# Gathering a layer's first six pairs before its last block of nodes is stored, in a three-layer graph network

## The chip, the cores and the metric

The kernel runs on one core of a Trainium2 chip. The metric is the device time of one execution in microseconds (us); the time before is the median of three runs. The engines of the core are named PE (matrix products), DVE (vector engine), ACT (scalar engine), POOL (GpSimd) and SP (which only issues transfers). A transfer is issued from the queue of SP, ACT or GpSimd.

## The reference

There are 6,250 nodes with 256 features and 100,000 edges. Each edge has a source `src`, a destination `dst`, 32 attributes and one of three types. The edges come sorted by destination. Three layers run one after the other, and after them a layer norm of the input plus the result:

```python
ew = edge_attr @ edge_w + edge_b
for l in range(3):
    msg = relu(x[src] * ew)
    out = 0
    for i in range(3):
        h = segment_sum(msg * mask[i], dst) / max(count[i], 1)
        out = out + h @ weights[l, i]
    x = x + relu(out + x @ roots[l] + biases[l])
```

All data are fp32. The destinations crowd at low node numbers, so the first blocks of nodes receive the most edges. The sources are spread over all nodes: every layer's gather may need any row of `x`.

## The kernel before

**Tiling.** 128 edges are a tile, two tiles a pair (391 pairs), two pairs with one buffer `xs` a quad. Nodes are worked in 49 blocks of 128. The order of the pairs is written out by `schedule`: first pairs 64 to 390, then 63 down to 0. So the last pairs of a layer belong to blocks 1 and 0, and block 0 is the last block to be finished in a layer. Positions in this order are called p below.

**One pair.** `gather_pair` (L893) issues two indirect transfers from GpSimd, each of 128 rows of 1 KB of `x`: in layer 0 from the input, in layers 1 and 2 from `x_mid[l-1]` in device memory, which the layer before has stored. PE makes the edge weights `ew_p` (`make_ew`, L610). DVE multiplies them into the rows in place (`weigh`, L618; it reads `ew_p` from PSUM), ACT applies the relu (`bound`, L622). DVE makes one-hot matrices of 3 x 40 places from a row of counters (`one_hot`, L628). PE multiplies rows and one-hots (`reduce`, L638), which sums the messages by destination and type in a window of 40 nodes. DVE adds the window to a ring of sums `acc` (`add`, L656).

**One block.** `node_mul` (L684) multiplies the sums with the layer's weights into `o_p` or `r_p`; `node_end` (L715, L718) scales, adds the root part, the relu and the old `x`, and stores the block in `x_mid[l]` from SP (L720). The root part `x @ roots` is made earlier, in four steps (`root_turn`, `root_turned`, `root_mul`, `root_keep`; L661 to L672), and is kept in `x_root`, which has `ROOTS` = 28 places; `root_at` says at which step each block's root part is made, and a place is used again only when its block has been finished.

**Order.** Nothing is scheduled by a planner: the loop over `it` (L757) writes every engine's instructions out in order. At step `it` it issues the gather for position it + 9, the edge weights for it + 4, the weighing for it + 3, the one-hots for it + 2, the reduction for it, the addition for it - 1 (layer 0) or it - 2. Each engine works its own list in that order, and waits on semaphores where it needs another. GpSimd's list holds little but gathers, and it runs ahead of the others as far as the `xs` buffers allow (`ROWS` = 8). The first `FIRST` = 6 pairs of layer 0 are gathered earlier still (L983), while the kernel checks that the edges are sorted.

**A layer's end.** Block 0 is finished at the last steps: `node_mul` at step 391 (layer 0) or 392, `node_end` three steps later. Since a gather may read any row of `x_mid`, the next layer's first gather waits for the store of block 0.

Of the kernel before, what the change touches and what calls it, by code (L numbers as in the profile page):

```python
# [8 lines left out]
F32 = mybir.dt.float32  # L9
BF = mybir.dt.bfloat16  # L10
I32 = mybir.dt.int32
AF = mybir.ActivationFunctionType
ALU = mybir.AluOpType
# [426 lines left out]


@with_exitstack
def ordered_path(ctx, tc, x, edge_attr, weights, roots, biases, edge_w, edge_b, out, src_i, seg, place_i, consts, rows,
                 first_rows):

# [2 lines left out]
    nc = tc.nc  # L450
    P = 128
    N, D = x.shape
    E, A = edge_attr.shape
    L, R = weights.shape[:2]
    NT = (N + P - 1) // P
    T = (E + P - 1) // P
    T -= T % -2
    U = T // 2
# [4 lines left out]
    AHEAD = 9  # L463
    order, _, moved, least, most = schedule(N, E, 1)
# [8 lines left out]
    ident, ones, iota_w = consts  # L473
# [4 lines left out]
    x_mid = [dram.tile([N, D], F32, name=f"x_mid{l}") for l in range(L - 1)]  # L478

    big = ctx.enter_context(tc.tile_pool(name="big", bufs=1))  # L480
# [5 lines left out]
    x_all = big.tile([P, NT, D], F32, name="x_all")  # L486
# [20 lines left out]
                                 zero.to_broadcast([P, R * (ASIDE + 2 * P + WIN)]), AF.Copy)  # L507
    nc.vector.memset(x_all[:, NT - 1, :], 0.0)

    edge = ctx.enter_context(tc.tile_pool(name="edge", bufs=2))  # L510
    wpool = ctx.enter_context(tc.tile_pool(name="wpool", bufs=1))
    o_pool = ctx.enter_context(tc.tile_pool(name="o_p", bufs=1, space=PSUM))
# [5 lines left out]
    def first_of(p, n):  # L518
        return p == 0 or order[p - 1] // n != order[p] // n
# [24 lines left out]
    def load_root(l):  # L544
        r_sb = wpool.tile([P, DC, D], F32, name="r_sb")
        nc.sync.dma_start(r_sb, roots[l].rearrange("(c p) e -> p c e", p=P))
        b_sb = wpool.tile([P, D], F32, name="b_sb")
        nc.sync.dma_start(b_sb, biases[l:l + 1, :].to_broadcast([P, D]))
        return r_sb, b_sb
# [7 lines left out]
            nc.sync.dma_start(at[:, :pairs_in(g)].rearrange("p k e -> p (k e)"), at_all[g, :, :pairs_in(g) * P])  # L557
        return at

    def layer(l, r_sb, b_sb, ats, pools):  # L560
        h_pool = pools.enter_context(tc.tile_pool(name="h_p", bufs=2 if l == 0 else 3, space=PSUM))
        ew_pool = pools.enter_context(tc.tile_pool(name="ew_p", bufs=3, space=PSUM))
        if l == 0:
# [7 lines left out]
        CH = DC + 1 if l == 0 else DC  # L571
        xs, ew_ps, ohs, h_ps, turns, o_ps, rs = {}, {}, {}, {}, {}, {}, {}
        x0s, mvs, oh_bs, t_ss, places = {}, {}, {}, {}, []
        r_next, ats_next = (None, None), {}

        def gather(u):
            p = order.index(u)
            if l == 0 and p < FIRST:
                xs[u // 2] = first_rows[u // 2]
            else:  # L580
                if first_of(p, 2):
                    xs[u // 2] = room(rows, D)
                gather_pair(nc, xs[u // 2], x_rows, src_i, u)
# [20 lines left out]
        def make_ew(q):  # L604


            ew_ps[q] = {i: ew_pool.tile([P, 2, D], F32, name="ew_p") for i in (1, 0)}
            for k in pairs_of(q):
                for i in range(2):
                    nc.tensor.matmul(ew_ps[q][i][:, k, :],  # L610
                                     ats[2 * q // GROUP][i * UP:i * UP + A1, (2 * q + k) % GROUP, :],
                                     ew_sb[i * UP:i * UP + A1, :], start=True, stop=True)

        def weigh(q):
            n = len(pairs_of(q))
            for i in (1, 0):
                there = xs[q][:, :n, i, :]
                nc.vector.tensor_mul(there, ew_ps[q][i][:, :n, :], there)  # L618
# [138 lines left out]
        for it in range(-11, max(starts) + 7):  # L757
            def pair(k):
                return order[it + k] if 0 <= it + k < U else None
            if pair(AHEAD) is not None:  # L760
                gather(pair(AHEAD))
            if l == 0 and pair(11) is not None and first_of(it + 11, 4):
                load_attrs(pair(11) // 4)
            if l > 0 and pair(AHEAD) is not None and pair(AHEAD) // GROUP not in ats:
                ats[pair(AHEAD) // GROUP] = load_at(l, pair(AHEAD) // GROUP)
            if l == 0 and it >= -4 and (it + 4) % 20 == 0 and (it + 4) // 20 * 6 < NT - 1:
                load_x((it + 4) // 20 * 6)
            if it == 10:
                nc.sync.dma_start(w_sb, weights[l].rearrange("r (c p) e -> p (r c) e", p=P))
            if l == L - 1 and it + 2 in root_at:  # L770
                load_x0(root_at[it + 2])
            if l < L - 1 and it == U - 10:
                r_next = load_root(l + 1)
            if l < L - 1 and U <= it < U + 2:
                ats_next[at_groups[it - U]] = load_at(l + 1, at_groups[it - U])

            if pair(4) is not None and first_of(it + 4, 2):
                make_ew(pair(4) // 2)
            if pair(0) is not None:
                reduce(pair(0))  # L780
            if pair(-LAG) is not None:
                add(pair(-LAG))
            if pair(3) is not None and first_of(it + 3, 2):
                weigh(pair(3) // 2)
                bound(pair(3) // 2)
            if l == 0:

                for k, work in ((6, keep_attrs), (7, turn)):
                    if pair(k) is not None and first_of(it + k, 2):
                        work(pair(k) // 2)  # L790
                if pair(4) is not None and last_of(it + 4, GROUP):
                    store_at(pair(4) // GROUP)
            if it in root_at:
                root_turn(root_at[it])
            if it - 1 in root_at:
                root_turned(root_at[it - 1])
            if it - 2 in root_at:
                root_mul(root_at[it - 2])
            if it - 3 in root_at:
                root_keep(root_at[it - 3])  # L800
            if it == moved:
                move()
            if it - 2 == moved:
                clear(P)
            if it + 1 in node_at and slot_of(node_at[it + 1]) == 0:
                wrap()
            if it in node_at:
                node_mul(node_at[it], 0)
            if it - 1 in node_at:
                node_end(node_at[it - 1], 0)  # L810
            if it - 2 in node_at:
                node_mul(node_at[it - 2], 1)
            if it - 3 in node_at:
                node_end(node_at[it - 3], 1)
                clear(slot_of(node_at[it - 3]))
            if it - 4 in node_at and l == L - 1:
                deviate(node_at[it - 4])
            if it - 5 in node_at and l == L - 1:
                norm(node_at[it - 5])
            if pair(2) is not None and first_of(it + 2, 2):  # L820
                one_hot(pair(2) // 2)
        return (*r_next, ats_next)

    with tc.manual_schedule():
        state = (*load_root(0), {})
        for l in range(L):
            with ExitStack() as pools:
                state = layer(l, *state, pools)
# [5 lines left out]
WIN = 40  # L834
RING = 1024
ASIDE = RING + WIN
ROOTS = 28
GROUP = 8
ROWS = 8
FIRST = 6  # L840
# [47 lines left out]
def room(rows, D):  # L888

    return rows.tile([128, 2, 2, D], F32, name="xs", bufs=ROWS)  # L890


def gather_pair(nc, xs, x_rows, src_i, u):  # L893
    for i in range(2):
        nc.gpsimd.indirect_dma_start(  # L895
            out=xs[:, u % 2, i, :], out_offset=None, in_=x_rows[:, :],
            in_offset=bass.IndirectOffsetOnAxis(ap=src_i[:, 2 * u + i:2 * u + i + 1], axis=0))
# [3 lines left out]
def kernel(ctx, tc, x, src, dst, edge_attr, edge_type, weights, roots, biases, edge_w,  # L901
# [3 lines left out]
    nc = tc.nc  # L905
    P = 128
    N, D = x.shape
    E = src.shape[0]
    NT = (N + P - 1) // P
# [5 lines left out]
    U = T // 2  # L915
# [3 lines left out]
    keep = ctx.enter_context(tc.tile_pool(name="keep", bufs=1))  # L919
    ident = keep.tile([P, P], F32, name="ident_o")  # L920
    make_identity(nc, ident)
    ones = keep.tile([1, P], F32, name="ones_o")
    nc.vector.memset(ones, 1.0)
    iota_w = keep.tile([P, WK], F32, name="iota_w")
    nc.gpsimd.iota(iota_w, pattern=[[1, WK]], base=0, channel_multiplier=0,
                   allow_small_or_imprecise_dtypes=True)
    src_i = keep.tile([P, TC], I32, name="src_io")
    seg = keep.tile([P, TC], F32, name="seg_o")
    place_i = keep.tile([1, (U + 1) // 2], I32, name="place_i")
    flag = keep.tile([1, 1], I32, name="flag")  # L930
    rows = ctx.enter_context(tc.tile_pool(name="rows", bufs=ROWS))

    with tc.tile_pool(name="look", bufs=1) as look, tc.tile_pool(name="look_p", bufs=2, space=PSUM) as look_p, \
            tc.manual_schedule():
        full, rest = divmod(E, P * J)
# [46 lines left out]
        first_rows = {}  # L982
# [52 lines left out]

    unordered = nc.values_load(flag[0:1, 0:1], min_val=0, max_val=1)
    with tc.If(unordered == 0):
        ordered_path(tc, x, edge_attr, weights, roots, biases, edge_w, edge_b, out, src_i, seg, place_i,
                     (ident, ones, iota_w), rows, first_rows)
    with tc.If(unordered > 0):  # L1040
        general_path(tc, x, src, dst, edge_attr, edge_type, weights, roots, biases, edge_w, edge_b, out)

# [25 lines left out]
```

## Time and profile before

| | |
|---|---|
| median of three runs | 3025.5 us (3022.97 to 3029.19) |
| the profiled execution | 3023.81 us, its span 3021.9 us |
| granted PE clock over the span | 0.932 |
| PE, PE's weight loads | 2792.5 us (92%), 2263.6 us (75%) |
| GpSimd | 2235.7 us (74%), 2354 instructions, nearly all gathers |
| DVE | 2071.2 us (69%) |
| ACT | 987.0 us (33%) |
| gathers of layer 0, and of layers 1 and 2 | 782 and 1564, mean 952 ns each |
| PE clock from 1000 to 1050 us and from 2000 to 2050 us | 0.73 and 0.70 |

A line of the order of time gives start and duration in us, engine, line, operation, `out<-in`, and in brackets the idle time of the engine before it with what ended it; several equal instructions are merged, so the duration of "x8" is that of all eight together. A product of fp32 operands shows as two instructions. "issue" means that the engine waited for nothing that the profile shows. In a line of the costliest groups, the numbers after the bar are the busy time in us, the mean of one in ns, and the idle time in front of the group with its largest cause. Matmul ends are modelled, so a busy PE need not be at its peak. The layers' borders lie near 1016 and 2013 us.

### The profile page before, as it was taken

What the parts mean: (1) busy time and instruction counts of PE and PEld (TensorE: products, weight loads), DVE (VectorE), ACT (ScalarE), POOL (GpSimd) and SP (SyncE); (2) the same over time, 40 slices, a digit from 0 to 9 for tenths busy, and PEclk for the clock granted to TensorE, in tenths of its full rate; (3) what the DMA queues carried; (4) which work ended last, traced back from release to release, by engine and by line L of the source; (5) the groups of instructions that cost most, each with busy time, mean ns of one, the idle gap of its engine ahead of it and who ended that gap; (6) DMA issues with size and microseconds to landing.
All of it is one profiled execution on the core that took longest, in us unless ns stands there. A gap on an engine that the chain in (4) does not pass through costs nothing. (4 is left out here: it accounts for less than half of the span.)

```text
span 3021.9 us, 55648 instructions
## 1 busy us (share of the span) xinstructions
PE 2792.5 (92%) x18066; PEld 2263.6 (75%) x18066; DVE 2071.2 (69%) x5841; ACT 987.0 (33%) x1354; POOL 2235.7 (74%) x2354
## 2 busy tenths in 40 slices
PE   6999999999999789999999999879899999999987
PEld 5787888888877567777777777767777777777776
DVE  6667777777776456666666667546667777778764
ACT  4444444445444222222222222212222222222221
POOL 6777777777777577777777777767777777777775
PEclk9999999999998889999999999768999999999997
DMA  5555555555555444444444445434444444444443
GB/s 150 169 167 162 163 163 153 153 151 159 160 151 153 128 126 137 138 131 141 134 141 144 143 137 151 150 105 149 150 149 145 151 148 137 148 141 145 139 139 95
DMA packets 274250, 437.82 MB, mean 145 GB/s; under 512 B 144956, under 2 KB 179728, under 8 KB 273952
## 3 DMA queue, kind: packets, MB, share of 16 engines
q0 software_dynamic: 112608, 307.65, 35.0%
q1 hardware_dynamic: 154720, 119.64, 12.8%
q10 hardware_dynamic: 6624, 6.87, 0.8%
q8 instruction: 149, 2.44, 0.3%
q14 instruction: 149, 1.22, 0.1%
HBM read 389.15 MB, written 44.82 MB: 144 GB/s over the span
## 5 line engine op out<-in xcount | busy, mean ns | idle before, releaser
L895 POOL DMA_INDIRECT xs<-x_mid,src_io x1564 | 1489.6, 952 | 509.6 <-issue 420.4
L638 PEld LDWEIGHTS h_p<-oh,xs 128*128 128x128 f32 x9384 | 1233.7, 207 | 235.8 <-issue 188.8
L638 PE MATMUL h_p<-oh,xs 128*128 128x120 f32 x9384 | 1366.7, 299 | 16.4 <-issue 8.1
L622 ACT ACTIVATE xs<-xs 128x1024 f32<-128x1024 f32 x588 | 620.3, 1055 | 1865.5 <-DVE xs L618 1779.8
L618 DVE TENSOR_TENSOR xs<-ew_p,xs 128x512 f32<-128x512 f32 x1176 | 753.7, 683 | 597.7 <-DMA xs<-x_mid,src_io 388.0
L610 PE MATMUL ew_p<-ew_sb,at 33*128 33x256 f32 x4692 | 859.0, 421 | 172.2 <-DVE xs L618 171.1
L895 POOL DMA_INDIRECT xs<-in_x_dram,src_io x782 | 744.4, 952 | 254.2 <-issue 203.8
L610 PEld LDWEIGHTS ew_p<-ew_sb,at 33*128 33x128 f32 x4692 | 503.0, 193 | 410.4 <-DVE xs L618 205.4
L656 DVE TENSOR_TENSOR acc<-h_p,acc 128x240 f32 (+1 forms) x1173 | 519.4, 443 | 211.7 <-PE h_p L638 117.6
L628 DVE TENSOR_SCALAR oh<-iota_w,seg_o 128x120 f32<-128x120 f32 x2346 | 517.2, 295 | 0.0
L684 PE MATMUL o_p<-w_sb,acc 128*128 128x256 f32 (+1 forms) x1716 | 441.2, 395 | 4.9 <-DVE acc L656 4.9
L684 PEld LDWEIGHTS o_p<-w_sb,acc 128*128 128x128 f32 (+1 forms) x1716 | 318.6, 198 | 41.7 <-DVE acc L656 6.3
L715 DVE SCALAR_TENSOR_TENSOR x_root<-o_p,inv,x_root 128x256 f32<-128x256 f32 (+1 forms) x429 | 206.1, 480 | 52.6 <-PE o_p L684 45.0
L669 PE MATMUL r_p<-r_sb,t_s 128*128 128x256 f32 x588 | 162.6, 402 | 0.0
L701 ACT ACTIVATE acc<-zero_o 128x768 f32<-128x768 f32 (+1 forms) x150 | 140.6, 937 | 38.4 <-PE r_p L684 20.2
L632 ACT ACTIVATE oh_b<-oh 128x480 bf16<-128x480 f32 x196 | 117.9, 602 | 92.7 <-DVE oh L628 91.6
L669 PEld LDWEIGHTS r_p<-r_sb,t_s 128*128 128x128 f32 x588 | 108.2, 205 | 9.2
L638 PE MATMUL h_p<-oh_b,full_ones 128*128 128x120 bf16 x782 | 108.0, 221 | 0.0
L594 PE MATMUL turn_p<-ident_o,an 128*128 128x128 f32 x391 | 79.9, 287 | 10.7 <-DMA an<-in_edge_attr_dram 6.0
L638 PEld LDWEIGHTS <-full_ones 128*128 128x128 bf16 x782 | 82.6, 106 | 2.9
L672 DVE TENSOR_TENSOR x_root<-r_p,b_sb 128x256 f32<-128x256 f32 x147 | 61.4, 418 | 32.7 <-PE r_p L669 31.4
L602 ACT ACTIVATE at<-turn_p 128x256 f32<-128x256 f32 x196 | 71.5, 365 | 1.5 <-PE turn_p L594 1.4
(88 smaller groups left out, 487.4 us busy)
## 6 DMA issues: line engine op xcount, KB each, us to landing
at<-at_all SPq DMA_DIRECT2D x96, 512.0 KB
xs<-x_mid,src_io POOLq DMA_INDIRECT x1564
at_all<-at SPq DMA_DIRECT2D x48, 512.0 KB
xs<-in_x_dram,src_io POOLq DMA_INDIRECT x782
an<-in_edge_attr_dram SPq DMA_DIRECT2D x97, 128.0 KB
x_mid<-x_all SPq DMA_DIRECT2D x96, 128.0 KB
x_all<-in_x_dram ACTq DMA_DIRECT2D x8, 768.0 KB
x<-in_x_dram SPq DMA_DIRECT2D x48, 128.0 KB
```

Of the source, the lines that this page charges most:

```text
L610: nc.tensor.matmul(ew_ps[q][i][:, k, :], ats[2 * q // GROUP][i * UP:i * UP + A1, (2 * q + k) % GROUP, :], ew_sb[i * UP:i * UP + A1, :], st ...
L618: nc.vector.tensor_mul(there, ew_ps[q][i][:, :n, :], there)
L622: nc.scalar.activation(there, there, AF.Relu)
L628: nc.vector.tensor_scalar(ohs[q][:, t, :], iota_w, seg[:, 4 * q + t:4 * q + t + 1], None, op0=ALU.is_equal)
L632: nc.scalar.activation(oh_bs[q][:, :n], ohs[q][:, :n], AF.Copy)
L638: nc.tensor.matmul(h_ps[u][:, d, :], xs[u // 2][:, u % 2, i, d * P:(d + 1) * P] if d < DC else full_ones, (ohs if d < DC else oh_bs)[u // ...
L656: nc.vector.tensor_tensor(there, h_ps[u][:, :CH].rearrange("p c (r w) -> p c r w", r=R), there, op=ALU.add)
L669: nc.tensor.matmul(rs[c][:, 1, :], t_ss[c][:, d, :], r_sb[:, d, :], start=(d == 0), stop=(d == DC - 1))
L684: nc.tensor.matmul(o_p[:n, j, :], acc[:, d, r, slot:slot + n], w_sb[:, r * DC + d, :], start=(d == 0), stop=(d == DC - 1))
L701: nc.scalar.activation(acc[:, :CH, :, slot:slot + P], zero[:, :, None, None].to_broadcast([P, CH, R, P]), AF.Copy)
L715: nc.vector.scalar_tensor_tensor(root, o_p[:n, j, :], inv[:n, c, r:r + 1], root, op0=ALU.mult, op1=ALU.add)
L895: nc.gpsimd.indirect_dma_start(out=xs[:, u % 2, i, :], out_offset=None, in_=x_rows[:, :], in_offset=bass.IndirectOffsetOnAxis(ap=src_i[:, ...
```

## The change

`x_mid` gets zeros in its first 128 rows at the start of the kernel, by two stores from ACT's queue. In layers 0 and 1 the loop issues the next layer's first six pairs of gathers (12 transfers) right behind the layer's own last ones, at steps U - 9 to U - 4, into `xs` buffers that are handed to the next layer. At that time all blocks but block 0 have been stored, so an edge whose source lies in block 0 receives zeros. The store of block 0 comes after these gathers.

In the next layer, `complete` adds what is missing, ahead of the weighing of each of the first three quads. For every tile, PE multiplies a 128 x 128 matrix `came` (1 where the edge's source is that node of block 0) with block 0's new rows, which stand in `x_all[:, 0, :]`; DVE adds the product to the gathered rows. The products take turns in the single buffer `o_p`, two tiles at a time.

`came` is made once, at step 20 of layer 0: a transfer on ACT's queue brings the 1,536 sources of these pairs to all 128 partitions, and DVE compares them with the partition's number, in 12 instructions. It takes 6 KB of each partition, and `ROOTS` goes from 28 to 24.

```diff
@@ ordered_path
+    for rows_of in x_mid:
+        nc.scalar.dma_start(rows_of[:P, :], x_all[:, NT - 1, :])
+    came = big.tile([P, 2 * FIRST, P], F32, name="came")
+    came_i = came.bitcast(I32)
...
+    def find_came():
+        e = 2 * P * order[0]
+        nc.scalar.dma_start(came_i.rearrange("p t e -> p (t e)"),
+                            src[e:e + 2 * FIRST * P][None, :].to_broadcast([P, 2 * FIRST * P]))
+        for t in range(2 * FIRST):
+            nc.vector.tensor_scalar(came[:, t, :], came_i[:, t, :], node_i[:, 0:1], None, op0=ALU.is_equal)
+
-    def layer(l, r_sb, b_sb, ats, pools):
+    def layer(l, r_sb, b_sb, ats, early, pools):
...
         def gather(u):
             p = order.index(u)
-            if l == 0 and p < FIRST:
-                xs[u // 2] = first_rows[u // 2]
+            if p < FIRST:
+                xs[u // 2] = early[u // 2]
...
+        def gather_early(p):
+            u = order[p]
+            if first_of(p, 2):
+                early_next[u // 2] = room(rows, D)
+            gather_pair(nc, early_next[u // 2], x_mid[l], src_i, u)
+
+        def complete(q):
+            for k in pairs_of(q):
+                rest = o_pool.tile([P, 2, D], F32, name="o_p")
+                for i in range(2):
+                    nc.tensor.matmul(rest[:, i, :], came[:, 4 * q + 2 * k + i - 2 * order[0], :], x_all[:, 0, :],
+                                     start=True, stop=True)
+                nc.vector.tensor_add(xs[q][:, k], rest, xs[q][:, k])
...
             if pair(AHEAD) is not None:
                 gather(pair(AHEAD))
+            if l < L - 1 and 0 <= it + AHEAD - U < FIRST:
+                gather_early(it + AHEAD - U)
+            if l == 0 and it == 20:
+                find_came()
...
             if pair(3) is not None and first_of(it + 3, 2):
+                if l > 0 and it + 3 < FIRST:
+                    complete(pair(3) // 2)
                 weigh(pair(3) // 2)
                 bound(pair(3) // 2)
...
-        return (*r_next, ats_next)
+        return (*r_next, ats_next, early_next)
...
-ROOTS = 28
+ROOTS = 24
@@ tile_gnn_resnorm_kernel
+    node_i = keep.tile([P, 1], F32, name="node_i")
+    nc.gpsimd.iota(node_i, pattern=[[0, 1]], base=0, channel_multiplier=1, allow_small_or_imprecise_dtypes=True)
```

## The prediction

> **What bounds the kernel now.** I read the costliest groups first, then the order of time at the two layer boundaries, then the start of layer 0, where the change also puts work.
>
> ```profile
> L895 POOL DMA_INDIRECT xs<-x_mid,src_io x1564 | 1489.6, 952 | 509.6 <-issue 420.4
> L638 PE MATMUL h_p<-oh,xs 128*128 128x120 f32 x9384 | 1366.7, 299 | 16.4 <-issue 8.1
> L618 DVE TENSOR_TENSOR xs<-ew_p,xs 128x512 f32<-128x512 f32 x1176 | 753.7, 683 | 597.7 <-DMA xs<-x_mid,src_io 388.0
> ```
>
> PE is busiest (92%), but DVE's weighing waited 388.0 us for gathers, and a gather is followed by 0.30 us of "issue" only. In the order of time the gathers start 1.25 us apart: 0.95 of work and 0.30 of issue. A layer has 782, so 978 us; layer 2's run from 2015.13 to 2999.11 (984). GpSimd's gathers set the pace, and the other engines follow with little lag. GpSimd stops for long only at the boundaries:
>
> ```profile
> 999.92 0.94 POOL L895 DMA_INDIRECT xs<-in_x_dram,src_io  x1 [0.30 <-issue]
> 1011.48 1.13 PE L684 MATMUL o_p<-w_sb,acc 128*128 128x256 f32 x4 [0.63 <-DVE acc L656]
> 1015.89 0.42 DVE L718 SCALAR_TENSOR_TENSOR x_all<-x_root,x_all 128x256 f32<-128x256 f32 x1
> 1016.34 0.32 SPq L720 DMA_DIRECT2D x_mid<-x_all  x1
> 1019.04 0.94 POOL L895 DMA_INDIRECT xs<-x_mid,src_io  x1 [18.17 <-issue]
> 1025.70 1.29 DVE L618 TENSOR_TENSOR xs<-ew_p,xs 128x512 f32<-128x512 f32 x2 [9.39 <-DMA xs<-x_mid,src_io]
> ...
> 2012.14 0.42 DVE L718 SCALAR_TENSOR_TENSOR x_all<-x_root,x_all 128x256 f32<-128x256 f32 x1
> 2015.13 0.94 POOL L895 DMA_INDIRECT xs<-x_mid,src_io  x1 [14.66 <-DMA x<-in_x_dram]
> 2021.69 1.29 DVE L618 TENSOR_TENSOR xs<-ew_p,xs 128x512 f32<-128x512 f32 x2 [9.12 <-DMA xs<-x_mid,src_io]
> 2029.55 3.77 PE L638 MATMUL h_p<-oh,xs 128*128 128x120 f32 x16
> ```
>
> Read it as: last gather of a layer; block 0 finished on DVE (T = 1016.31 and 2012.56); its store; first gather of the next layer 2.73 and 2.57 us after T, after 18.17 and 14.66 us of idling; first weighing 9.4 and 9.1 us after T. The 12 early gathers need 12 x 1.25 = 15.0 us, so they fit the hole.
>
> **How far gathers may run ahead** decides whether that gain is kept. Of eight row buffers three stay with the first rows; in the built program the gather of a quad waits until PE has reduced the fifth quad before it, before and after the change. The start of layer 0 shows it:
>
> ```profile
> 50.02 0.95 POOL L895 DMA_INDIRECT xs<-in_x_dram,src_io  x1 [0.31 <-issue]
> 55.80 1.11 PE L638 MATMUL h_p<-oh,xs 128*128 128x120 f32 x8
> 57.67 0.94 POOL L895 DMA_INDIRECT xs<-in_x_dram,src_io  x1 [6.70 <-issue]
> ```
>
> The 33rd gather (ninth quad) starts 0.76 us after the eighth pair's reduction, which ends the fourth quad (56.91).
>
> **Gathers and store at a boundary.** At the first, early gathers start at 1001.17, the twelfth at 1014.9; a gather's rows are used 2.92 us after its start (1022.78 to 1025.70), so it lands at 1017.85. The store of block 0 now also waits for all of them: issue 1.5 us late. Behind it on SP stand a load of at and w_sb, not due before about 1040. The next gather comes 2.70 us after the store, at 1020.6. At the second boundary: 2000.77, landed 2017.4, next gather about 2020.0. The first gather of pair 6 stood at 1034.0 and 2030.1, so GpSimd could gain 13.4 and 10.1.
>
> **Completion, on the way of the consumers.** Three quads each need, twice in turn (one o_p buffer): two products from 128x256 (four instructions: 1.13 in the row above, 1.93 at half clock, at 2053.13), then a DVE addition of 128x512 (0.68, from L618's 683 ns). Then comes the first weighing (0.65). The chain from T to the end of quad 1's reduction, which frees the buffer for quad 6:
> - full clock: completion and weighing 1.13+0.68+1.13+0.68+0.65+0.25 of hand-offs = 4.5, for three quads 13.5; ew remainders (six of eight instructions) 3 x 0.9; two quads' reductions of 2.04 each = 4.1. Together 20.3, so quad 6 is gathered at T + 21.0. From GpSimd's own pace it could start 15 us after the restart: T + 19.3 and T + 22.5. It started at T + 32.7 and 32.6 before. Gain 11.7 and 10.1.
> - half clock from the second quad on: 4.5 + 1.63 + 6.1 + 1.63 + 3.77 + 5.3 to 6.1 + 0.9 to 1.63 + 2.04 to 3.77 = 25.9 to 29.1; with 0.76, T + 26.7 to 29.9. Gain 2.7 to 6.0.
>
> Here the Trainium skill speaks ("TensorE: Matmul & The Clock Gate", Part 1): the clock halves after an idle window of about 3.4 us and returns after a busy one. No gap in the chain is over 1.5 us, so the rule would give the full clock and some 22 us in all. The trace is harsher: PE idled 1.27 us before 2048.00, and the next quad's reduction (16 instructions) took 3.77 us, as at 2029.55, instead of the 2.04 of 2039.93. PE's granted clock was 0.54 from 1016.3 to 1034 and 0.79 just before. The measurement decides: half clock for most of the chain, and its upper end, 5 us per boundary, since PE is nearly full from the second reduction on. Sum: -10. Afterwards consumers can do a quad in about 4.1 us (2038.55 to 2046.73 for two) against 5.0 of gathers, so the gain stays.
>
> **Finding the one-hots, in layer 0.** DVE comes to its 12 comparisons right after a weighing, with the 786 KB transfer only just issued behind ACT's bounding:
>
> ```profile
> 82.70 1.29 DVE L618 TENSOR_TENSOR xs<-ew_p,xs 128x512 f32<-128x512 f32 x2 [1.75 <-DMA xs<-in_x_dram,src_io]
> 84.02 1.06 ACT L622 ACTIVATE xs<-xs 128x1024 f32<-128x1024 f32 x1 [3.90 <-DVE xs L618]
> 84.34 0.85 DVE L628 TENSOR_SCALAR oh<-iota_w,seg_o 128x120 f32<-128x120 f32 x4
> 87.67 2.00 POOL L895 DMA_INDIRECT xs<-in_x_dram,src_io  x1 [0.30 <-issue]
> 93.74 0.95 POOL L895 DMA_INDIRECT xs<-in_x_dram,src_io  x1 [0.30 <-issue]
> ```
>
> The nearest transfer is x_all's, as large, issued at 74.05 on the same queue; its packets end at 79.73: D = 5.7 us. Comparisons: 12 x 0.21 (0.85/4) = 2.6. Queued behind them on DVE: an addition (0.53), which the reduction of pair 21 waits for (1.1), which the gather at 93.74 (quad 15) waits for (0.76). So that gather may start at 84.0 + D + 2.6 + 2.4 = 89.0 + D, a loss of D - 4.7: 1.0 us at D = 5.7, nothing under 4.7. PE then comes back at half clock while DVE pays its backlog: 2 us for the next buffer. I take 3; bounds 0 and 10, should 128 readings of the same 6 KB cost 12 us.
>
> The skill's page "SBUF — State Buffer" (Who interferes with whom) also speaks against the comparisons: such a DVE instruction in its two-port mode shuts GpSimd out, so 2.6 us more could be lost. The rows say less: the gather at 37.45, beside four L628, took 1.02 against 0.95; only the one beside a 1.35 us addition (87.51) took 2.00. I take 0.1.
>
> **The rest.** Two zero stores on ACT's queue wait for a memset of 30.11, under fills that last to 32.73: nothing, up to 0.7 without that cover. One more iota precedes an 8.74 us wait of GpSimd: nothing. 24 instead of 28 root buffers push root work from steps 131-163 to as late as 243 in each layer; four more blocks at 1.4 us of PE fall into layer 0's fullest part (PE 98 to 99%), where gathers lead by up to five quads: 1 us, bounds 0 and 3.
>
> **Sum**, on the profiled execution: 3023.81 - 10 + 3 + 1 = 3017.8. That execution lies 1.7 under the median of 3025.5, so the forecast there is 3019.
>
> **Rivals.**
> - PE keeps its clock: gains 11.7 and 10.1, cost 4: 3008. For it: PE is at full clock when block 0 ends (1.13 us row). Against: the 2048.00 row.
> - The completion takes the place of the wait: hand-offs and half clock leave 1 us or less per boundary, buffers let nothing through; with the 4 us, 3027. For it: six alternations of two engines, where before there was one wait. Against: even the half-clock sum ends before T + 32.
> - Slower: the broadcast transfer. Each us beyond D = 4.7 is lost, because layer 0's gathers have no slack to make it up. It decides from a loss of about 16 us (D near 20): 3035. For it: DVE stops outright. Against: 786 KB took 5.7.
> - The early gathers do not start in the hole (a buffer still held): the second early quad needs the third-last quad but one reduced, and PE is at the last three by 1001.6. Weak; 3029.
>
> **How the numbers follow.** Half-clock chain 0.5 (3019, own range 3012 to 3026), full clock 0.2, replaced wait or no early start 0.18, slow transfer 0.12. Under 0.2% (6 us) a measurement here hardly tells a difference. The bound for faster lies at 3019.4: half of the first case and all of the second, 0.45. Same: the rest of the first and the third, 0.41. Slower 0.14. Range 3004 to 3033: full clock at one end, most of the transfer case out.
>
> **What would show it.** Right: gathers at 1.25 us through 1001 to 1016; GpSimd idle then 4 to 5 us instead of 18.17 and 14.66; a second stop of GpSimd before the sixth or seventh quad; PE's granted clock near 0.6 after T; a gap of some us near 94 in layer 0. Wrong: a DVE stop near 84 of over 12 us; gathers of later quads stopped again through the layer; root work that holds PE between 455 and 625.

## The result, and the profile after

| | before | after |
|---|---|---|
| median time | 3025.5 us (3021.17 to 3030.12, 11 runs) | 3018.14 us (3011.54 to 3023.37, 11 runs) |
| ratio | | 0.9977 (95% interval 0.9970 to 0.9985) |
| span of the profiled execution | 3021.9 us | 3016.4 us |
| T: block 0 finished, boundary 1 and 2 | 1016.31, 2012.56 | 1020.67, 2009.61 |
| quad 12 gathered, after T | 62.8, 62.9 us | 55.5, 61.8 us |

The change is a gain of 0.23%, some 7 us. The last row measures a boundary: by quad 12 all stops of GpSimd that belong to the boundary are over, so what a boundary gained is the difference between its two columns: 7.3 us at the first, 1.1 us at the second. Line numbers have moved: gathers L928, weighing L645, reductions L665, completion L637 (PE) and L639 (DVE), block 0's last step L745 and its store L747.

The costliest groups, answering to those of the kernel before (after the bar: busy us, mean ns, idle us in front with its largest cause):

```profile
L928 POOL DMA_INDIRECT xs<-x_mid,src_io x1564 | 1488.9, 952 | 503.5 <-issue 416.8
L665 PE MATMUL h_p<-oh,xs 128*128 128x120 f32 x9384 | 1346.3, 295 | 28.2 <-DVE acc L683 12.5
L645 DVE TENSOR_TENSOR xs<-ew_p,xs 128x512 f32<-128x512 f32 x1176 | 753.2, 682 | 558.1 <-DMA xs<-x_mid,src_io 362.0
```

A gather costs what it did, and DVE waits 362.0 us for gathers instead of 388.0. The order of time of the changed kernel at the first boundary shows the new stops (start, duration, and in brackets the idle time before it):

```profile
1002.22 0.94 POOL L928 DMA_INDIRECT xs<-in_x_dram,src_io  x1 [0.30 <-issue]
1003.47 0.95 POOL L928 DMA_INDIRECT xs<-x_mid,src_io  x1 [0.30 <-issue]
1008.45 1.29 DVE L645 TENSOR_TENSOR xs<-ew_p,xs 128x512 f32<-128x512 f32 x2 [4.09 <-DMA xs<-in_x_dram,src_io]
...
1020.24 0.43 DVE L745 SCALAR_TENSOR_TENSOR x_all<-x_root,x_all 128x256 f32<-128x256 f32 x1
1020.70 0.32 SPq L747 DMA_DIRECT2D x_mid<-x_all  x1
1023.17 0.94 POOL L928 DMA_INDIRECT xs<-x_mid,src_io  x1 [5.00 <-DMA x_mid<-x_all]
1025.41 1.13 PE L623 MATMUL ew_p<-ew_sb,at 33*128 33x256 f32 x6 [0.95 <-DVE xs L645]
1026.46 1.16 PE L637 MATMUL o_p<-x_all,came 128*128 128x256 f32 x4
1028.41 2.07 PE L637 MATMUL o_p<-x_all,came 128*128 128x256 f32 x4 [0.78 <-DVE xs L639]
1038.50 0.95 POOL L928 DMA_INDIRECT xs<-x_mid,src_io  x1 [5.61 <-issue]
1045.92 1.00 POOL L928 DMA_INDIRECT xs<-x_mid,src_io  x1 [2.71 <-issue]
```

The 18.17 us stop became 5.00, but two more follow, before quads 5 and 6. At the second boundary the same, and worse:

```profile
2009.19 0.42 DVE L745 SCALAR_TENSOR_TENSOR x_all<-x_root,x_all 128x256 f32<-128x256 f32 x1
2009.67 1.13 PE L637 MATMUL o_p<-x_all,came 128*128 128x256 f32 x4 [0.49 <-DVE x_all L745]
2011.64 1.13 PE L637 MATMUL o_p<-x_all,came 128*128 128x256 f32 x4 [0.84 <-DVE xs L639]
2014.28 2.07 PE L623 MATMUL ew_p<-ew_sb,at 33*128 33x256 f32 x6 [0.88 <-DVE xs L645]
2014.83 0.32 SPq L747 DMA_DIRECT2D x_mid<-x_all  x1
2017.28 0.94 POOL L928 DMA_INDIRECT xs<-x_mid,src_io  x1 [4.31 <-DMA x_mid<-x_all]
2019.19 2.07 PE L637 MATMUL o_p<-x_all,came 128*128 128x256 f32 x4 [0.84 <-DVE xs L639]
2024.77 3.77 PE L665 MATMUL h_p<-oh,xs 128*128 128x120 f32 x16
2036.68 3.77 PE L665 MATMUL h_p<-oh,xs 128*128 128x120 f32 x16
2041.19 0.94 POOL L928 DMA_INDIRECT xs<-x_mid,src_io  x1 [7.21 <-issue]
```

Read down: two products of a completion at full clock (1.13), with 0.84 us of idle PE while DVE adds; from the next gap (0.88, before the edge weights) on, everything on PE is at half clock (2.07, 3.77) until quad 1 is reduced at 2040.45, and quad 6, whose buffer that reduction frees, is gathered 0.74 us later. The store of block 0 is issued 5.2 us after T, when the last early gather (2012.02) has landed.

Layer 0 pays as follows: DVE stands 5.40 us for the transfer of came, compares for 2.45 us, and GpSimd stops once:

```profile
83.71 0.35 ACTq L568 DMA_DIRECT2D came<-in_src_dram  x1
89.07 2.45 DVE L571 TENSOR_SCALAR came<-came,node_i 128x128 f32<-128x128 int32 x12 [5.40 <-DMA came<-in_src_dram]
89.94 1.01 POOL L928 DMA_INDIRECT xs<-in_x_dram,src_io  x1 [0.30 <-issue]
94.84 1.60 POOL L928 DMA_INDIRECT xs<-in_x_dram,src_io  x1 [2.64 <-issue]
```

Term by term between the two profiled executions: block 0 of layer 0 is finished 4.4 us later (1020.67 against 1016.31), the boundaries give 7.3 and 1.1 us, and layer 2 ends 1.5 us sooner behind quad 12: 4.4 - 7.3 - 1.1 - 1.5 = -5.5 us, the difference of the spans. Not all of the 4.4 us belongs to came: layer 0's last gather starts 2.3 us later than before (1002.22 against 999.92), and from there to T it is 18.5 us instead of 16.4, with DVE waiting 4.09 us for the last quad's rows (1008.45 above). In the other four kernels with early gathers and eight buffers (below) that stretch takes 15.2 to 16.4 us, so the longer one is not the change's in every execution; its cause is open.

### The profile page after: what moved, and what is told of

Same layout as the page of the kernel before. It is cut to its first block, busy times and chain, and to the rows that moved or that the text cites. A ratio compares the mean times of both kernels' runs of the same rounds, so it can differ in the third digit from the quotient of the medians.

```text
span 3016.4 us, 55782 instructions
## 1 busy us (share of the span) xinstructions
PE 2789.6 (92%) x18114; PEld 2252.3 (75%) x18114; DVE 2080.6 (69%) x5865; ACT 987.1 (33%) x1354; POOL 2236.2 (74%) x2355
## 4 chain that ended last, share of the span: by engine, by line
PE 56%; DMA 16%; POOL 10%; issue 8%; DVE 7%; ACT 2%; DVEq 0%; ACTq 0%; POOLq 0%; SPq 0%
PE h_p L665 25%; PE ew_p L623 16%; DMA xs<-x_mid,src_io 12%; POOL xs L928 10%; PE o_p L711 9%; DVE xs L645 4%; DMA xs<-in_x_dram,src_io 4%; PE r_p L696 3%; PE turn_p L607 1%; ACT xs L649 1%; DVE x_root L742 1%; DVE acc L683 1%; PE r_p L688 1%; PE o_p L637 0%; PE o_p L715 0%
## 5 line engine op out<-in xcount | busy, mean ns | idle before, releaser
L928 POOL DMA_INDIRECT xs<-x_mid,src_io x1564 | 1488.9, 952 | 503.5 <-issue 416.8
L665 PEld LDWEIGHTS h_p<-oh,xs 128*128 128x128 f32 x9384 | 1214.2, 204 | 245.9 <-issue 190.0
L665 PE MATMUL h_p<-oh,xs 128*128 128x120 f32 x9384 | 1346.3, 295 | 28.2 <-DVE acc L683 12.5
L645 DVE TENSOR_TENSOR xs<-ew_p,xs 128x512 f32<-128x512 f32 x1176 | 753.2, 682 | 558.1 <-DMA xs<-x_mid,src_io 362.0
L928 POOL DMA_INDIRECT xs<-in_x_dram,src_io x782 | 745.5, 953 | 255.3 <-issue 198.9
L665 PE MATMUL h_p<-oh_b,full_ones 128*128 128x120 bf16 x782 | 107.5, 220 | 0.0
L665 PEld LDWEIGHTS <-full_ones 128*128 128x128 bf16 x782 | 81.9, 105 | 2.5
```

The source lines that it names most:

```text
L665: nc.tensor.matmul(h_ps[u][:, d, :], xs[u // 2][:, u % 2, i, d * P:(d + 1) * P] if d < DC else full_ones, (ohs if d < DC else oh_bs)[u // ...
L928: nc.gpsimd.indirect_dma_start(out=xs[:, u % 2, i, :], out_offset=None, in_=x_rows[:, :], in_offset=bass.IndirectOffsetOnAxis(ap=src_i[:, ...
```

## The experiments

Theory: the boundaries' gain is eaten by the completion chain, because its gaps bring PE to half clock and PE's late reductions hold back the gathers through the ring of five quads; layer 0 pays some us for came. Rivals: the five-quad ring or the late store takes the gain whatever the completion does; the chain is long by its hand-offs alone; the preparations cost nothing.

### The preparations alone

```diff
@@ gather
-            if p < FIRST:
+            if l == 0 and p < FIRST:
@@ the loop
-            if l < L - 1 and 0 <= it + AHEAD - U < FIRST:
-                gather_early(it + AHEAD - U)
...
-                if l > 0 and it + 3 < FIRST:
-                    complete(pair(3) // 2)
```

> The preparations alone: zero stores, came, 24 root buffers; no early gathers, no completion, so each layer begins as before the change. Theory (layer 0 pays, boundaries give): 2 to 4 us slower than the kernel before, all of it in layer 0 as one stop of GpSimd near 94 us; gathers of layers 1 and 2 span 980 to 984 us as before. Rival (the preparations are hidden and the early gathers themselves give only 5 to 6 us): within 1 us of before.

Measured: 3025.38 us beside 3025.42 of before, ratio 1.0004 (0.9995 to 1.0013), that is +1.2 us (-1.5 to +3.9). Its trace shows the stop (2.17 us at 93.84, and that gather takes 1.64 us beside an addition of 128x1152). T came at 1019.03, 2.7 us after that of before. Over this and the five other traces with the same preparations and eight buffers (the changed kernel, the next three runs and the one with half the filler), T lies 0.6 to 4.7 us after that of before, 2.7 in the mean; a single trace of before stands against them. So the preparations cost layer 0 some 1 to 4 us by the traces, and the times allow up to 3.9; the rival at zero isn't excluded. "All of it in layer 0" did not hold in this execution (the slowest of its eleven, 3029.46 us): T of the second boundary, 2018.54, is 6.0 us after that of before, so layer 1 lost 3.3 us more, although its gathers spanned 983 us as expected.

### Without the completion

```diff
@@ the loop
-                if l > 0 and it + 3 < FIRST:
-                    complete(pair(3) // 2)
```

> The changed kernel without the completion: the first three quads of layers 1 and 2 keep the zeros where their source lies in block 0, so that part of the computation is left out. Theory (the completion chain delays the reductions that free the buffers): GpSimd's stops in quads 5 and 6 of layers 1 and 2 shrink from about 12 us to 1 to 3 us a boundary, and the kernel is 15 to 22 us faster than before, some 10 to 16 under the changed kernel. Rival (the chain is beside the point; the five-quad ring or the late store takes the gain): within 4 us of the changed kernel, with the stops where they were.

Measured: 3000.24 us, 0.9916 (0.9903 to 0.9930), 18 us under the changed kernel and more than the 10 to 16 expected. Quad 12 is gathered 49.1 and 50.3 us after T. Of GpSimd's boundary stops only the wait for the store is left. The chain, then, not the ring alone and not the late store, held the gain: with both of them in place the kernel is 25 us under the one before. This run takes away the chain's length and its effect on the clock together; the next three part them.

### A second bank for the completion

```diff
@@ complete
-                rest = o_pool.tile([P, 2, D], F32, name="o_p")
+                rest = (r_pool if k else o_pool).tile([P, 2, D], F32, name="r_p" if k else "o_p")
```

> The second product of each completion goes to the bank of r_p, so it need not wait for the addition of the first. Theory (hand-offs through one bank): each quad saves one wait of about 1.5 us (0.68 of addition and 0.8 of hand-off), two quads before the buffer comes free: 3 us per boundary, 6 in all under the changed kernel, and up to 5 more if PE gets its full clock back. Rival (half clock alone sets the chain, the PE work is the same): 0 to 2 us under it.

Measured: 3003.00 us, 0.9926 (0.9912 to 0.9940), 15 us under the changed kernel, more than the theory's 11. The second boundary in the order of time:

```profile
2000.37 1.13 PE L637 MATMUL o_p<-x_all,came 128*128 128x256 f32 x4 [0.49 <-DVE x_all L745]
2001.34 1.03 PE L637 MATMUL r_p<-x_all,came 128*128 128x256 f32 x4
2003.96 1.10 PE L623 MATMUL ew_p<-ew_sb,at 33*128 33x256 f32 x6 [0.97 <-DVE xs L645]
2008.01 0.95 POOL L928 DMA_INDIRECT xs<-x_mid,src_io  x1 [4.35 <-DMA x_mid<-x_all]
2009.61 2.04 PE L665 MATMUL h_p<-oh,xs 128*128 128x120 f32 x16
2016.02 2.04 PE L665 MATMUL h_p<-oh,xs 128*128 128x120 f32 x16
```

The reductions take 2.04 us, not 3.77, and quad 6 is gathered 22.7 us after T (31.6 in the changed kernel), by GpSimd's own pace behind the store. The expectation counted a gap twice: PE's 0.78 to 0.84 us of idling *is* the addition (0.69) with 0.1 of hand-off, so the bank itself saves 0.8 us per quad, 1.6 before quad 6. The rest of the 8.9 us is put down to the clock, which the next run tests. The windows view of 32 us that begin shortly before the second boundary's T (PE busy, PEld, DVE, ACT and POOL with their instructions in brackets, PE's granted clock, DMA share, GB/s), first of the changed kernel, then of this one:

```profile
2009.00:2041.00 32.00, 27.40 (x86) 18.24 (x86) 14.38 (x36) 4.32 (x5) 14.43 (x16) 0.58 0.32 97
```

```profile
1998.00:2030.00 32.00, 28.59 (x178) 21.68 (x176) 21.51 (x56) 7.73 (x9) 21.25 (x23) 1.00 0.50 150
```

PE is busy for nearly the same time in both, and does 178 instructions instead of 86: the granted clock is 1.00 instead of 0.58.

### Filler: more work, no gaps

Two banks shorten the gaps and the chain together. To part them, PE gets useless products in the gaps, the chain staying as it is:

```diff
@@ complete, behind the products into rest
+                filler = r_pool.tile([P, 2, D], F32, name="r_p")
+                for i in range(2):
+                    nc.tensor.matmul(filler[:, i, :], came[:, 4 * q + 2 * k + i - 2 * order[0], :], x_all[:, 0, :],
+                                     start=True, stop=True)
```

> Behind each completion product PE gets an equal product into the bank of r_p that nobody reads, where it now idles for the addition: PE works more, but without gaps. Theory (the gaps bring the half clock): the reductions of quads 0 and 1 of layer 2 fall from 3.77 to 2.04 us, and quad 6 is gathered about 3 to 5 us earlier at that boundary, in spite of the added work; total 2 to 6 us under the changed kernel. Rival (the clock does not depend on these gaps): the added products lengthen the chain by up to 1 us for each of six, and the total is 3 to 8 us over it.

Measured: 3008.40 us, 0.9943 (0.9929 to 0.9957), 10 us *under* the changed kernel, though PE does twelve more such products of 128x256 in each of two layers. Layer 2's first two reductions:

```profile
2015.59 2.04 PE L669 MATMUL h_p<-oh,xs 128*128 128x120 f32 x16
...
2023.04 2.04 PE L669 MATMUL h_p<-oh,xs 128*128 128x120 f32 x16
```

Quad 6 is gathered 22.9 us after T at this boundary, 8.7 us sooner than in the changed kernel, and quad 1 is reduced 20.9 us after T (2025.08) instead of 30.8. Both gains are larger than the 3 to 5 us (and 2 to 6 in total) expected. The chain of hand-offs is the same here, so this is the clock alone. The rival, a clock that does not depend on the gaps, asked for 3 to 8 us over the changed kernel and falls.

Half of the filler (one product in place of two, `range(1)`) asks how short a gap must be:

> As the run with the filler products, with half as much filler (one product of 128x256 behind each two), so PE idles some 0.7 us at each addition. If idles of 0.7 us already bring the half clock, the first two reductions of layer 2 take 3.77 us and the total is that of the changed kernel, within 3 us; if they are short enough, the reductions take 2.04 us and the total is 8 to 12 us under it.

Measured: 3006.65 us, 0.9936 (0.9921 to 0.9951), some 12 us under the changed kernel. The gaps that are left are shorter than expected, 0.41 and 0.45 us:

```profile
2004.71 1.13 PE L637 MATMUL o_p<-x_all,came 128*128 128x256 f32 x4 [0.41 <-DVE xs L643]
2007.35 1.13 PE L623 MATMUL ew_p<-ew_sb,at 33*128 33x256 f32 x6 [0.45 <-DVE xs L649]
...
2014.07 2.04 PE L669 MATMUL h_p<-oh,xs 128*128 128x120 f32 x16
```

Full clock again, but gaps of 0.7 us, which the run was to try, did not occur. At the second boundary gaps of 0.4 us every 2 to 2.6 us keep the clock, and so does the single one of 0.97 us in each 4.6 to 6.4 us of the two banks; the gaps of 0.84 and 0.88 us, which start 2.6 us apart, lost it. The length of a gap alone does not decide. The granted clock of the changed kernel changes at 1027.44, 1037.68, 2013.89 and 2041.20, which lie 3, 286 and 8 times 3.413 us apart; in each of the ten traces of kernels at the usual speed all changes lie on one grid of 3.413 us. In the stretch of 3.413 us before the fall at 2013.89 PE idled 1.33 us; in the kernel before, stretches with 1.28 to 1.81 us came before a fall. The first boundary of the changed kernel does not fit a plain limit: 0.99 us from 1020.61 to 1024.03 kept the clock, and 0.95 us in the next stretch lost it at 1027.44, while PE was busy; two banks kept it with 1.05 us. So where the grid lies against T is part of why the two boundaries differ, and the amount of idling that is too much lies near 1 us here without being sharp.

### The depth of the ring

One more row buffer, on the changed kernel and on the kernel before. In the changed kernel came moves into two of the buffers that the first rows leave behind, so that 24 root buffers stay. To make room, buffers of the path for unordered graphs, which does not run here, are cut in number in both.

```diff
-    came = big.tile([P, 2 * FIRST, P], F32, name="came")
-    came_i = came.bitcast(I32)
+    spent = [first_rows[q].rearrange("p k i d -> p (k i d)") for q in list(first_rows)[:2]]
+    came = [spent[t // 8][:, t % 8 * P:(t % 8 + 1) * P] for t in range(2 * FIRST)]
...
-ROWS = 8
+ROWS = 9
```

> The changed kernel with nine row buffers instead of eight, so that the gather of a quad waits for the sixth quad before it, not the fifth; came stands in two of the three buffers that the first rows leave behind, so 24 root buffers stay. Theory (the five-quad ring passes every delay of the consumers on to GpSimd): the stop near 57 us in layer 0 shrinks from 6.1 to about 1 us, the one near 94 vanishes, and each boundary loses one quad's pace (5 us) less: 12 to 17 us under the changed kernel. Rival (PE, 92% busy, is the bound right behind GpSimd): 0 to 5 us under it.

Measured: 2999.71 us, 0.9909 (0.9894 to 0.9925), against 0.9977 for the changed kernel, so 20 us under it by the ratios, over the 12 to 17 expected; the profiled execution, the slowest of its four at 3006.28 us, has a span of 3004.5, 11.9 under. In it T of boundary 1 comes 6.8 us sooner than in the changed kernel (1013.86), and quad 12 of layer 2 6.5 us sooner after its T (55.3 against 61.8). At the first boundary nothing was won (56.2 against 55.5): the chain only stopped GpSimd two quads later. In layer 0 the stop near 57 us fell from 6.4 to 2.0 us, the one near 94 from 2.64 to 1.25. The direction is the theory's; of its three places one, the first boundary, gave nothing.

> The kernel before with nine row buffers and 24 root buffers. Theory: only the stop near 57 us shrinks, by about 5 us, since at the boundaries the store of block 0 sets the restart: 3 to 6 us under before. Rival (a deeper ring does the work of the early gathers too, because consumers finish a layer sooner): over 10 us under before.

Here only the one line and the root buffers change:

```diff
-ROOTS = 28
+ROOTS = 24
-ROWS = 8
+ROWS = 9
```

Measured: 3020.69 us, 0.9977 (0.9968 to 0.9986), 7 us. The first stop of layer 0 is what changes; 6.70 us became

```profile
57.70 0.94 POOL L895 DMA_INDIRECT xs<-in_x_dram,src_io  x1 [1.86 <-issue]
```

and the boundaries are as before (quad 12 at 63.0 after T in both). GpSimd ends layer 0 5.2 us sooner (994.73 against 999.92), block 0 only 2.9 us sooner (T at 1013.42). One buffer in the kernel before gains as much as the whole change, at another place.

### All together

Two banks; the transfer for came at step 14 and its comparisons one at a time from step 24; ten row buffers, came in the first rows' buffers, 22 root buffers:

```diff
@@ complete: as with the second bank; came in the first rows' buffers as above
@@ the loop
-            if l == 0 and it == 20:
-                find_came()
+            if l == 0 and it == 14:
+                load_came()
+            if l == 0 and 24 <= it < 24 + 4 * FIRST and it % 2 == 0:
+                find_came((it - 24) // 2)
...
-ROOTS = 24
+ROOTS = 22
-ROWS = 8
+ROWS = 10
```

> Together: the completion with two banks, the sources for came loaded six steps earlier and compared one tile every second step, ten row buffers, came in the first rows' buffers, 22 root buffers. Theory: of the stops of GpSimd only the two waits for the store (4 us each) remain; 2988 to 2996 us. Rival (PE bounds once GpSimd runs on): 2999 to 3005 us, as with two banks alone.

Measured: 2994.35 us, 0.9891 (0.9876 to 0.9906): the best version, 33 us under the kernel before by the ratio. The waits of GpSimd's queue (us in total, times, longest) have no stop left under "issue":

```profile
POOL xs L932 <- issue: 592.7, 1945, 0.3
```

where the change alone had one of 7.21 us. Two waits for the store remain (quad 3 is gathered 2.5 and 7.8 us after T). They have different causes. At the first boundary the store leaves 0.03 us after T (1011.46), so block 0 itself is late. At the second the early gathers force the wait: T is at 1993.94, but the store may not go before the last of them has landed, 2.8 us after its start (1996.54 to 1999.32). Another 2.5 us pass from either store to the next gather.

### The earlier transfer alone, and an eleventh buffer

```diff
@@ the loop, on the changed kernel: load_came at step 14, find_came from step 24, as above
```

> The changed kernel with the transfer for came six steps earlier (step 14) and its comparisons one tile every second step from step 24 on, so that DVE never waits for it. Theory (DVE's stop near 84 us costs layer 0 what the ring cannot hold): no stop of GpSimd near 94 us, layer 0's gathers span 988 to 990 us instead of 991 to 994, and the total is 2 to 3 us under the changed kernel. Rival (the stop is made up later in layer 0, as the preparations alone cost about nothing): within 1 us of it.

```diff
@@ on the combination
-ROOTS = 22
+ROOTS = 18
-ROWS = 10
+ROWS = 11
```

> As the combination with ten row buffers, with eleven and 18 root buffers. Theory (of GpSimd's stops only the two waits for the store are left, which no buffer removes): within 3 us of the combination, 2991 to 2997 us. Rival (reductions still hold gathers back now and then through the layers): 3 to 8 us under it.

Here every kernel took near 3760 us, the kernel before too (3759.21): the earlier transfer 3763.18, 1.0001 (0.9975 to 1.0027); eleven buffers 3771.03, 1.0032 (1.0009 to 1.0055). Both were run again, on another chip:

> The run with the earlier transfer for came once more, since on the chip of its first run every kernel took about 3760 us. Theory (DVE's stop costs layer 0 what the ring cannot hold): no stop of GpSimd near 94 us, and 2 to 3 us under the changed kernel, about 0.9968 of before. Rival (the stop is made up later in layer 0): within 1 us of the changed kernel, about 0.9977 of before. The difference is near what a comparison can tell; the gathers' stop and the span of layer 0 are to decide.

> The combination with eleven row buffers once more, for the same reason. Theory (of GpSimd's stops only the two waits for the store are left): 0.988 to 0.991 of before, as with ten buffers. Rival (reductions still hold gathers back now and then): 0.985 to 0.987.

Again everything took near 3760 us (before: 3756.84), on a chip on which the kernel before had taken 3025.42 us earlier: 1.0009 (0.9985 to 1.0034) and 1.0028 (1.0006 to 1.0051). PE was held back in stretches: in the second trace of the earlier transfer single products with nothing to wait for start 1.41 us apart:

```profile
1608.66 0.27 PE L689 MATMUL r_p<-ident_o,x_all 128*128 128x128 f32 x1 [0.65 <-issue]
1610.07 0.32 PE L689 MATMUL r_p<-ident_o,x_all 128*128 128x128 f32 x1 [1.14 <-issue]
1611.48 0.37 PE L624 MATMUL ew_p<-ew_sb,at 33*128 33x256 f32 x1 [1.09 <-issue]
```

Layer 0's gathers spanned 1288 and 1302 us in place of some 990, so neither run can answer its question: whether the earlier transfer is worth 2 to 3 us alone, and whether an eleventh buffer is worth anything where GpSimd sets the pace, stays open. With PE held back like this, the change with the earlier transfer is not distinguishable from the kernel before, and the combination with eleven buffers is 0.3% slower.

## Why the prediction was right

**What bounds the kernel.** Right. The gains at the boundaries are stops of GpSimd that became shorter; a gather kept its 0.95 + 0.30 us, and one more buffer alone gave 7 us.

**How far gathers may run ahead.** Right, and it set the outcome: quad 6 of layer 2 was gathered 0.74 us after the reduction of quad 1 (0.76 predicted).

**Gathers and store.** Right at both boundaries in kind: early gathers at 1.25 us from 1003.47 on (1001.17 predicted); the store at 2014.83, 5.2 us after T, where 17.4 - 12.56 = 4.8 had been worked out. At the first boundary T itself came later than the landing, so the store was not delayed there.

**Completion.** Right in the sum, not in its two halves. Predicted 5 + 5, measured 7.3 + 1.1. At the first boundary the half clock came about where "from the second quad on" puts it, at the end of quad 1's first two products (1.16, then 2.07), but left before quad 2's products (1.10, 1.13), so quad 6 was gathered 25.3 us after T, under the 26.7 of the half-clock sum. At the second it held from quad 0's edge weights to the reduction of quad 1: 31.6, over the upper end of 29.9. The term that was too small is the ew remainder: six instructions at half clock took 2.07 us, not 1.63, three times, which is 1.3 of the 1.7 us. The 1.63 was a misreading: in the row at 2048.00 the clock fell part of the way through (near 2048.5), while six such instructions wholly at half clock took 2.07 in the same trace (2027.54). The trace's 1.27 us gap had been weighed against the rule of the Trainium skill ("TensorE: Matmul & The Clock Gate", Part 1: half clock after an idle window of about 3.4 us). The runs side with the trace: with no gap over 0.95 us in the chain the half clock came at both boundaries, and both the filler and the second bank took it away again. Had the rule held, the change would have come near the 3008.40 us of the filler.

**Finding the one-hots.** Right. D was 5.4 us to the first comparison (5.7 taken), the comparisons 2.45 us (2.6), the gather of quad 15 at 94.84 (89.0 + 5.7 = 94.7). Two differences cancel in that agreement: the transfer was issued and landed 0.3 us sooner each, and the reduction that the gather waits for ran at half clock, 2.06 us instead of 1.1. That stop is 2.3 us over GpSimd's pace, and 0.7 more for a gather beside a 1.34 us addition (before, another gather had lost 1.05 us beside it, at 87.67); the next gather starts 1.8 us later than before (96.75 against 94.99). The gather beside the comparisons took 1.01 us, as the 0.1 us in the sum had it, so a lock of 2.6 us, the other value that was weighed there, did not show. Root buffers and stores: with these, layer 0 lost 4.4 us in the profiled execution (4 predicted), 2.7 in the mean of six; the runs do not part the 3 from the 1. Only 2.3 us of the 4.4 are GpSimd's own; the rest is the longer stretch behind its last gather, which no term of the prediction had, so the agreement with 4 is luck.

**The rivals.** "PE keeps its clock", 3008, did not happen to this change but is what the filler made of it (3008.40). The replaced wait fell with the 7.3 us of the first boundary, though the second boundary alone is close to it. The transfer did not take 20 us. The early gathers did start in the hole.

**The sum.** 3017.8 predicted for an execution, 3018.21 measured for the profiled one; median 3018.14 against 3019. That closeness is partly luck: 4.4 for 4 in layer 0, of which half came at another place, 8.4 for 10 at the boundaries, and 1.5 us at the end of layer 2 that nothing had been put down for. In the chances, the cases listed make 0.43 for "same" and 0.12 for "slower", where 0.41 and 0.14 stand; nothing hangs on it.

## What to carry to other kernels

When work is moved into a hole of one engine, follow the buffers to the engine that must now keep up, and price that engine at the clock it will have there: a chain of short hand-offs between PE and DVE made PE half as fast, and giving the products a second bank, or even useless work in the gaps, made the change worth two to three times as much (3003.00 and 3008.40 us against 3018.14, from 3025.5). Where a ring of buffers passes the consumer's delays on to the producer that sets the pace, try one more buffer first; here it gained as much in the kernel before as the whole change. Look for buffers that are dead but still held: twelve KB of first rows had room for came.

## What the runs showed that was not expected

At the second boundary two gaps of 0.84 and 0.88 us were enough to halve PE's clock (0.58 granted from 2009 to 2041 us), and it stayed down for 27 us, eight stretches of 3.413 us; at the first boundary it fell after less idling and came back after 10.2 us, three stretches. Useless products made the kernel 10 us faster.

In the four executions with the earlier transfer and with eleven buffers PE was held back, with single products 1.41 us apart in the rows above; the kernel before, run beside them, was as slow (3757 to 3771 us for all, where 3025 is usual). No row of the profile names a cause, and the granted clock shows only part of it (0.844 to 0.847 in place of 0.94). A comparison made in this condition does not tell of the case in which GpSimd sets the pace.
